# A two-layer graph attention network: layer 1's rows split among TensorE, VectorE and ScalarE by a search, its softmax moved, and the 41-row tile fetched row by row

## The chip, the cores and the metric

The kernel runs on one core of a Trainium2 chip. The metric is device time in microseconds (us) of one execution; lower is better. The engines are named as the profile names them: PE (TensorE, matmuls), DVE (VectorE), ACT (ScalarE), POOL (GpSimd, which here issues the gathers) and SP (SyncE, which issues the plain DMAs). Each engine works through its own instructions in the order in which the program lists them; semaphores order the engines against each other.

## The reference

The inputs are 10,000 nodes of 768 numbers, float32, and 170,000 edges, to which the reference adds a loop at every node. Two graph attention layers follow each other, each with a layer norm and a residual product:

```
def gat_conv(x, src, dst, W, a_src, a_dst, bias, heads, out_ch, concat):
    xl = (x @ W).reshape(n, heads, out_ch)
    alpha_src = einsum('nhc,hc->nh', xl, a_src); alpha_dst = einsum('nhc,hc->nh', xl, a_dst)
    e = leaky_relu(alpha_src[src] + alpha_dst[dst], 0.2)
    e = exp(e - segment_max(e, dst)[dst])
    alpha = e / (segment_sum(e, dst)[dst] + 1e-16)
    out = segment_sum(xl[src] * alpha[:, :, None], dst)
    ... # heads side by side (concat) or averaged
    return out + bias

h = relu(layer_norm(gat_conv(x, W1, ..., heads=4, out_ch=256, concat=True))) + x @ Wr1 + br1
h1 = h
h = layer_norm(gat_conv(h, W2, ..., heads=1, out_ch=768, concat=False)) + h1 @ Wr2 + br2
return layernorm(x + h)
```

So layer 1 has rows of 4 x 256 = 1024 numbers, layer 2 rows of 768.

## The kernel before

**Preparation and table.** The first part sorts the nodes by their number of edges and makes lists of neighbours, while PE multiplies all nodes by W1; the products, with the two logits of each head beside them, go to a table in DRAM (rows of 1033 numbers). The sorted nodes are cut into 79 tiles of 128. A tile of n rows needs n gathers: gather k fetches, for each of its 128 nodes, the table row of that node's k-th neighbour, one node on each partition. The tiles have 8 to 27 rows, and one has 41. They are worked on in the order 8, 10, 11, ... 26, 41, 27, 25, ... 9 rows; by number of tiles: one each of 8, 9, 10, 25, 26, 27 and 41 rows, three each of 11 and 12, five of 13, six of 14, eight of 15, seven of 16, eight of 17, seven each of 18 and 19, six of 20, four each of 21 and 22, two each of 23 and 24.

**Layer 1** (`ordered_layer1`) is what the change is about. Its instructions stand in the order written by hand. The gathered rows lie in a ring of 29 slots (`Ring`, `RING1`); `ring.fetch(q)` lists gathers on POOL up to row q, and a gather into a slot waits until whoever used the slot's old row is done. For each tile of up to 29 rows:

- `logits` (L477 to L489, DVE, with an exp on ACT, L485) makes the weights e of all of the tile's rows, for which all rows must have landed. `normalised` (L496 to L502, DVE) divides them by their sum. Both are called through the generator `weights_of(t + 1)` near the end of tile t: its first step, the logits, three rows before the end, its second one row later, and the rest at the start of the next tile, ahead of the table store.
- The first m rows of a tile (`on_pe`, at most `ON_PE1` = 4) are PE's: `summed` has ACT make a diagonal matrix of the weights for each row and head (L723, four a row), and PE multiplies the rows by them into `acc` in PSUM (L729; a matmul of float32 shows as two records).
- Of the other rows every fourth is DVE's alone: `weigh` multiplies and adds with four instructions (L519), onto `acc` in PSUM. The rest are shared: `multiply` has ACT multiply the row in place by its weights (L508, four instructions), running at most `LEAD` = 3 rows ahead, and DVE adds the result in one instruction (L515).
- At the start of the next tile DVE takes statistics of the finished `acc` (L572, L574), ACT makes the deviation of them (`sd`, L576 and L577), and DVE makes h in three instructions (L586, L588, L800). PE transposes x and h (L699), ACT copies the transposes out of PSUM (`xT`, `hT`, L700), and PE does the products x @ Wr1 (L171) and h @ W2 (L817). ACT copies the latter into `row` (L759), and SP stores it into layer 2's table (L761). The two halves of `row` and the transposes share two PSUM buffers (`half`).
- SP also stores h (L812) and x (L707) for layer 2; POOL gathers the next tile's x (`next_x`, `fetch_x`).

The 41-row tile doesn't fit the ring. `attend_parts` takes it in three groups of 13 or 14 rows, with a running maximum: four rows by PE into `sums`, the first third of the others by DVE alone, the rest shared; the earlier total is scaled by `fade` (L539, L542) when the maximum rises. At the end of a group DVE adds `sums` (L553), and only then the group's slots are fetched again:

```
                nc.vector.tensor_add(acc[:, :c], acc[:, :c], sums[:, :c])
                ring.fetch(hi + ring.size)
                continue
```

All work that is due in a tile (`due`: hT's copies, the product h @ W2, the next gather of x), and the product x @ Wr1, stand ahead of the first group.

**Layer 2** does the same with 768 numbers a row and a ring of 41 slots, in which every tile fits.

Of the kernel before, what the change touches and what calls it, by code (L numbers as in the profile page):

```python
# [28 lines left out]
F32 = mybir.dt.float32  # L29
# [6 lines left out]
P = 128  # L36
BANK = 512
# [10 lines left out]
RING2 = 41  # L48
LEAD = 3
DIAGONALS = 5  # L50
ON_PE2 = 512
SHARE = 4
ON_PE1 = 4
# [26 lines left out]
def gnn_kernel(ctx, tc, x, x_cols, src, dst, src_col, dst_col, W1, a_src1, a_dst1, b1, g1, be1, Wr1, br1,  # L80
# [441 lines left out]
    def attend_parts(small, ring, acc, h_, ad, bias, heads, dh, t, summed=None):  # L522
# [5 lines left out]
        top = total = None  # L528
        nc.vector.memset(acc[:, :c], 0.0)
        for lo, hi in zip(cuts, cuts[1:]):  # L530
# [5 lines left out]
            if top is not None:  # L536
                fade = small.tile([P, heads], F32, name="fade")
# [8 lines left out]
            if summed:  # L546
                sums, m = summed(lo, e)
                for q in range(lo + m, hi):
                    shared = q >= lo + m + (hi - lo - m) // 3
                    if shared:  # L550
                        multiply(ring.slot(q), e[:, q - lo], dh)
                    weigh(acc, ring.slot(q), e[:, q - lo], dh, shared=shared)
                nc.vector.tensor_add(acc[:, :c], acc[:, :c], sums[:, :c])  # L553
                ring.fetch(hi + ring.size)
                continue
            for q in range(lo, hi):
                shared = heads > 1 and (q - lo) % SHARE
                if shared:
                    multiply(ring.slot(q), e[:, q - lo], dh)
                weigh(acc, ring.slot(q), e[:, q - lo], dh, shared=shared)  # L560
                ring.fetch(q + 1 + ring.size)
        divided(small, h_, acc, total, bias, heads, dh)
# [115 lines left out]
    def ordered_layer1():  # L678
        nc.scalar.add_instruction(mybir.InstLoadActFuncSet(name=nc.get_next_instruction_name(), act_func_set_id=6, engine=nc.scalar.engine))
        with tc.tile_pool(name="b1", bufs=1) as pool, tc.tile_pool(name="small1", bufs=2) as small, \  # L680
# [5 lines left out]
            def fetch_x(t):  # L686
                xt = pool.tile([P, D0], F32, name="xt")
                gather(xt, x[:, :], nodes(t))
                return xt
# [13 lines left out]
            def from_x(t):  # L703

                xT = pool.tile([P, K0, P], F32, name="xT")
                moves = halves(xT, xt)
                nc.sync.dma_start(x_d[t], xt)  # L707
                return xT, moves
# [5 lines left out]
            def on_pe(t):  # L714


                return min(max(SLOTS[t] // 2 - 5, 1), ON_PE1, SLOTS[t])

            def summed(acc, diagonals, e, q, lo, hi, m):

                for k in range(lo, hi):
                    for i in range(H1):
                        nc.scalar.activation(diagonals[:, k * H1 + i, :], ident, AF.Copy,  # L723
                                             scale=e[:, k, i:i + 1])
                for k in range(lo, hi):
                    for i in range(H1):

                        c, d = i * DH1, (i + 1) * DH1
                        nc.tensor.matmul(acc[:, c:d], diagonals[:, k * H1 + i, :], ring.slot(q + k)[:, c:d],  # L729
                                         start=(k == 0 and c % BANK == 0),  # L730
                                         stop=(k == m - 1 and (d % BANK == 0 or d == C1)),
                                         skip_group_check=True)

            def weights_of(t):
# [6 lines left out]
                diagonals = pool.tile([P, ON_PE1 * H1, P], F32, name="diagonals")  # L741
                for lo, hi in ((0, min(m, 2)), (min(m, 2), m)):
                    summed(acc, diagonals, e, FIRST[t], lo, hi, m)
                    yield acc

            def shared(t, k):
                return (k - on_pe(t)) % SHARE > 0

# [19 lines left out]
            for t in range(NT + 1):  # L768
# [4 lines left out]
                if whole and not ready:  # L773
                    ahead = weights_of(t)
                    ready += itertools.islice(ahead, 2)
# [8 lines left out]
                if whole:  # L784
                    e, acc = ready
                if last:
                    r_before, means = last
                    stats = deviation(small, pieces(means[:, :C1], BANK))
                for _ in ahead:
                    pass  # L790
# [16 lines left out]
                if live and t:  # L807
                    r = product(xT, wr1, C1, ps_r)
# [26 lines left out]
                if live and not whole:  # L835
                    due(n)
# [4 lines left out]
                    def some(q, e):  # L841
                        m = min(ON_PE1, e.shape[1])
                        diagonals = pool.tile([P, ON_PE1 * H1, P], F32, name="diagonals")
                        summed(sums, diagonals, e, q, 0, m, m)
                        return sums, m

                    h = pool.tile([P, C1], F32, name="h")
                    attend_parts(small, ring, h, acc, ad, None, H1, DH1, t, some)
                ready = []
                ahead = iter(())  # L850
                if whole and t + 1 < NT and SLOTS[t + 1] + LEAD <= ring.size:
                    ahead = weights_of(t + 1)
                for k in range(n if whole else 0):
                    multiplied(k + 1 + LEAD)
                    if n - LEAD <= k < n - LEAD + 2:
                        ready += itertools.islice(ahead, 1)
# [5 lines left out]
                ready += itertools.islice(ahead, max(2 - len(ready), 0))  # L862
# [5 lines left out]
    def ordered_layer2():  # L868
        nonlocal ps_big
        with tc.tile_pool(name="b2", bufs=1) as pool, tc.tile_pool(name="small2", bufs=2) as small, \  # L870
# [61 lines left out]
            def residual(t):  # L932
# [4 lines left out]
                for c in range(0, C2, BANK):  # L937
# [3 lines left out]
                    for j in range(K1):  # L941
                        nc.tensor.matmul(r[:, c:d], hT[:, j, :], wr2[:, j, c:d], start=False,  # L942
                                         stop=(j == K1 - 1 and (d < C2 or not whole(t))),
# [340 lines left out]
```

## Time and profile before

| | |
|---|---|
| median of 7 runs | 5656.28 us (5637.28 to 5664.47) |
| the profiled execution | 5655.13 us, its span 5653.3 us |
| busy in the span | PE 4900.7 us (87%), DVE 4287.8 (76%), POOL 3228.4 (57%), PE's weight loads 2898.2 (51%), ACT 2810.3 (50%) |
| layer 1, by its first gather and its last tile's statistics | 892 to 3429 us from the span's start |
| moved by DMA | 1591.37 MB, mean 281 GB/s |
| DVE adds of shared rows, L515 | 801, mean 1230 ns |
| ACT multiplications, L508 | 3284, mean 508 ns (they overlap: 1338.2 us in all) |

Times are of one profiled execution, in us from the start of the span unless ns is said. In a list of groups or a timeline a line has the kernel's line, the engine, the operation, the tiles written and read, their shapes, the number of instructions, and in brackets the idle time of the engine just before, with what ended it. A stretch's line has its length, then for each engine busy us and the number of instructions, the clock that was granted to PE (1.00 is full), the mean busy share of the 16 DMA engines and GB/s. In the slices each digit is the busy share of one fortieth of the span, in tenths.

### The profile page before, as it was taken

How to read it: one execution, taken by the hardware profiler on the slowest of the kernel's cores; microseconds unless marked ns; L12 is line 12 of the kernel's file. 1: busy time of each engine (PE TensorE's matmuls, PEld its weight loads, DVE VectorE, ACT ScalarE, POOL GpSimd, SP SyncE). 2: the span in 40 equal slices, each digit the busy share in tenths (PEclk: the TensorE clock that was granted, in tenths of full speed). 3: DMA queues.
4: the chain of work that ended last, by engine and by line, in shares of the span. 5: the costliest groups of instructions: out<-in, count | busy, mean ns of one | idle time of the engine just before them, and what ended most of it. 6: DMA issues, size and time to landing. Idle time of an engine off the chain costs nothing. (4 is left out here: it accounts for less than half of the span.)

```text
span 5653.3 us, 59565 instructions
## 1 busy us (share of the span) xinstructions
PE 4900.7 (87%) x15188; PEld 2898.2 (51%) x15191; DVE 4287.8 (76%) x7729; ACT 2810.3 (50%) x8184; POOL 3228.4 (57%) x3159
## 2 busy tenths in 40 slices
PE   9999996999999865789999998998887747788898
PEld 3444443555555543455555555655555534455565
DVE  5783344999999886888899995886676656767787
ACT  3443344777787766777877762332222222222232
POOL 3447364556666655566665543666666656656663
PEclk9999997999999987899999999998888877888999
DMA  4333636999999986899999986998888878888885
GB/s 155 122 98 86 92 93 248 321 335 352 362 368 368 346 319 229 319 344 353 358 360 358 340 287 252 325 333 305 295 304 286 285 242 299 297 295 299 313 326 195
DMA packets 474306, 1591.37 MB, mean 281 GB/s; under 512 B 118327, under 2 KB 122487, under 8 KB 473958
## 3 DMA queue, kind: packets, MB, share of 16 engines
q0 software_dynamic: 322384, 1286.62, 64.3%
q1 hardware_dynamic: 149520, 297.43, 16.1%
q10 hardware_dynamic: 2054, 3.42, 0.2%
q8 instruction: 128, 2.10, 0.1%
q14 instruction: 220, 1.80, 0.1%
HBM read 1431.80 MB, written 177.29 MB: 285 GB/s over the span
## 5 line engine op out<-in xcount | busy, mean ns | idle before, releaser
L424 POOL DMA_INDIRECT ring<-table,slots x2675 | 2649.8, 991 | 1744.1 <-issue 527.6
L519 DVE SCALAR_TENSOR_TENSOR acc<-ring,e,acc 128x512 f32<-128x512 f32 (+1 forms) x2530 | 1578.0, 624 | 150.6 <-PE acc L729 48.7
L508 ACT ACTIVATE ring<-ring,e 128x256 f32<-128x256 f32 x3284 | 1338.2, 508 | 2.4 <-issue 2.2
L515 DVE TENSOR_TENSOR acc<-acc,ring 128x1024 f32<-128x1024 f32 x801 | 985.6, 1230 | 72.3 <-ACT ring L508 2.1
L942 PE MATMUL big<-wr,w 128*128 128x512 f32 (+1 forms) x2464 | 896.9, 508 | 161.1 <-issue 159.1
L928 PE MATMUL big<-ring,diagonals 128*128 128x256 f32 x2754 | 731.2, 424 | 189.9 <-issue 152.5
L171 PE MATMUL big<-w,xT 128*128 128x512 f32 x1896 | 827.4, 598 | 26.9 <-DMA w<-in_W_dram 10.0
L171 PE MATMUL big<-wr,xT 128*128 128x512 f32 x1896 | 834.8, 597 | 0.2 <-ACT xT L700 0.2
L817 PE MATMUL half<-w,hT 128*128 128x512 f32 (+1 forms) x2528 | 830.4, 486 | 0.0
L942 PEld LDWEIGHTS big<-wr,w 128*128 128x128 f32 x2464 | 487.6, 199 | 541.9 <-issue 510.0
L928 PEld LDWEIGHTS big<-ring,diagonals 128*128 128x128 f32 x2754 | 581.5, 214 | 343.1 <-issue 213.6
L927 ACT ACTIVATE diagonals<-ident,e 128x128 f32<-128x128 f32 x1377 | 423.9, 388 | 647.5 <-remote 274.4
L729 PE MATMUL acc<-ring,diagonals 128*128 128x256 f32 x1912 | 483.0, 411 | 220.6 <-ACT diagonals L723 200.5
L817 PEld LDWEIGHTS half<-w,hT 128*128 128x128 f32 x2528 | 477.8, 189 | 372.8 <-issue 327.2
L171 PEld LDWEIGHTS big<-w,xT 128*128 128x128 f32 x1896 | 362.9, 192 | 487.4 <-issue 469.6
L171 PEld LDWEIGHTS big<-wr,xT 128*128 128x128 f32 x1896 | 357.4, 192 | 421.3 <-issue 420.6
L729 PEld LDWEIGHTS acc<-ring,diagonals 128*128 128x128 f32 x1912 | 389.9, 207 | 306.1 <-ACT diagonals L723 218.5
L576 ACT ACTIVATE sd<-mv,eps 128x1 f32<-128x1 f32 x237 | 69.3, 293 | 706.4 <-DVE mv L574 450.2
L723 ACT ACTIVATE diagonals<-ident,e 128x128 f32<-128x128 f32 x956 | 292.8, 387 | 202.8 <-DVE e L499 138.6
L660 DVE TENSOR_TENSOR scr<-big,ad_b 128x1024 f32<-128x1024 f32 x79 | 96.7, 1224 | 381.5 <-ACT row L657 325.9
L665 POOL TENSOR_TENSOR row<-row,none 128x1024 f32<-128x1024 f32 x79 | 186.9, 2366 | 268.3 <-ACT row L657 264.9
L485 ACT ACTIVATE e<-e 128x68 f32<-128x68 f32 (+29 forms) x160 | 38.2, 239 | 574.3 <-DVE e L484 283.7
(172 smaller groups left out, 3629.6 us busy)
## 6 DMA issues: line engine op xcount, KB each, us to landing
ring<-table,slots POOLq DMA_INDIRECT x2675
table<-row SPq DMA_DIRECT2D x79, 516.0 KB
h_d<-hT SPq DMA_DIRECT2D x79, 512.0 KB
w<-h_d SPq DMA_DIRECT2D x77, 512.0 KB
table<-row SPq DMA_DIRECT2D x79, 385.0 KB
ring<-table SPq DMA_DIRECT2D x79, 385.0 KB
xT<-in_x_cols_dram SPq DMA_DIRECT2D x79, 384.0 KB
x_d<-xt SPq DMA_DIRECT2D x79, 384.0 KB
```

Source lines behind the costliest of these rows:

```text
L171: nc.tensor.matmul(p[:, c:e], aT[:, j, :], w[:, j, c:e], start=(j == 0), stop=(j == k - 1))
L424: nc.gpsimd.indirect_dma_start(out=to, out_offset=None, in_=table, in_offset=bass.IndirectOffsetOnAxis(ap=index, axis=0), **more)
L508: nc.scalar.activation(row[:, s], row[:, s], AF.Copy, scale=e[:, h:h + 1])
L515: nc.vector.tensor_add(acc[:, :c], acc[:, :c], row[:, :c])
L519: nc.vector.scalar_tensor_tensor(acc[:, s], row[:, s], e[:, h:h + 1], (acc if first is None else first)[:, s], op0=OP.mult, op1=OP.add)
L665: nc.gpsimd.tensor_add(row[:, :C1], row[:, :C1], b1_b)
L723: nc.scalar.activation(diagonals[:, k * H1 + i, :], ident, AF.Copy, scale=e[:, k, i:i + 1])
L729: nc.tensor.matmul(acc[:, c:d], diagonals[:, k * H1 + i, :], ring.slot(q + k)[:, c:d], start=(k == 0 and c % BANK == 0), stop=(k == m - 1 ...
L817: nc.tensor.matmul(q, hT[:, j, :], w2[:, j, c:c + q.shape[1]], start=(j == 0), stop=(j == K1 - 1))
L927: nc.scalar.activation(diagonals[:, k % G, :], ident, AF.Copy, scale=e[:, k, :])
L928: nc.tensor.matmul(to, diagonals[:, k % G, :], ring.slot(FIRST[t] + k)[:, ON_PE2:C2], start=False, stop=(k == n - 1), skip_group_check=True)
L942: nc.tensor.matmul(r[:, c:d], hT[:, j, :], wr2[:, j, c:d], start=False, stop=(j == K1 - 1 and (d < C2 or not whole(t))), skip_group_check= ...
```

## The change

In layer 1 a search replaces the fixed shares. For every number n of rows it tries all splits into rows of PE (`pe`), rows of DVE alone (`alone`) and shared rows (`both`), and takes the one with the least longest time of three linear costs:

```
+PE_FIXED, PE_ROW = 24.0, 1.86
+DVE_FIXED, DVE_ROW, DVE_SUM = 7.9, 2.15, 1.31
+ACT_FIXED, ACT_ROW, ACT_DIAGONAL = 4.0, 1.65, 1.21
...
+            def balanced(n):
+                def longest(pe, alone):
+                    both = n - pe - alone
+                    return max(PE_FIXED + PE_ROW * pe, DVE_FIXED + DVE_SUM * both + DVE_ROW * alone,
+                               ACT_FIXED + ACT_DIAGONAL * pe + ACT_ROW * both)
+                return min(((pe, alone) for pe in range(1, n) for alone in range(1, n - pe + 1)),
+                           key=lambda s: (longest(*s), s))
...
             def on_pe(t):
-                return min(max(SLOTS[t] // 2 - 5, 1), ON_PE1, SLOTS[t])
+                return split[SLOTS[t]][0]
...
             def shared(t, k):
-                return (k - on_pe(t)) % SHARE > 0
+                m, alone = split[SLOTS[t]]
+                return (k - m) * alone % (SLOTS[t] - m) >= alone
```

`summed` becomes a generator that does two rows a step, with two buffers of two rows' diagonals in place of one buffer of four rows'. The steps of `weights_of(t + 1)` are called at other rows:

```
+                begin = n
                 if whole and t + 1 < NT and SLOTS[t + 1] + LEAD <= ring.size:
+                    begin = min(max(n - EARLY, n + SLOTS[t + 1] - ring.size + EARLY), n - 2)
                     ahead = weights_of(t + 1)
                 for k in range(n if whole else 0):
                     multiplied(k + 1 + LEAD)
-                    if n - LEAD <= k < n - LEAD + 2:
-                        ready += itertools.islice(ahead, 1)
+                    if k == begin or k > begin + 1:
+                        step = list(itertools.islice(ahead, 1))
+                        ready += step[:2 - len(ready)]
```

(`EARLY` is 5.) At a tile's start, when its first sums were begun in the tile before, the rest of its diagonals and the first multiplications now stand ahead of the statistics; otherwise the normalisation and all sums stand behind them:

```
-                if whole:
+                if len(ready) == 2:
                     e, acc = ready
+                    for _ in ahead:
+                        pass
+                    multiplied(first + 2)
                 if last:
                     r_before, means = last
                     stats = deviation(small, pieces(means[:, :C1], BANK))
+                if whole and len(ready) < 2:
+                    if not ready:
+                        ahead = weights_of(t)
+                    ready += itertools.islice(ahead, 2 - len(ready))
+                    e, acc = ready
                 for _ in ahead:
                     pass
```

In the 41-row tile PE takes the last four rows of a group (the first four in the last group); `sums` is added in the next group, behind its logits; each row is fetched again as soon as it is listed as used; and the product x @ Wr1 stands behind group 1, the rest of the due work behind group 2 (`between`):

```
             if top is not None:
+                nc.vector.tensor_add(acc[:, :c], acc[:, :c], sums[:, :c])
...
+            m = min(ON_PE1, hi - lo - 1)
+            pe = lo if hi == cuts[-1] else hi - m
+            sums, steps = summed(e[:, pe - lo:], pe, m)
+            next(steps)
+            if pe == lo:
+                for _ in steps:
+                    pass
+            alone = [q for q in range(lo, hi) if not pe <= q < pe + m]
+            for k, q in enumerate(alone):
+                shared = k >= len(alone) // 3
                 if shared:
                     multiply(ring.slot(q), e[:, q - lo], dh)
+                if k == len(alone) // 3 + 1:
+                    for _ in steps:
+                        pass
                 weigh(acc, ring.slot(q), e[:, q - lo], dh, shared=shared)
                 ring.fetch(q + 1 + ring.size)
-        divided(small, h_, acc, total, bias, heads, dh)
+            ring.fetch(hi + ring.size)
+            between.pop(0)()
+        nc.vector.tensor_add(acc[:, :c], acc[:, :c], sums[:, :c])
+        divided(small, h_, acc, total, None, heads, dh)
```

SP's store of x moves from the next tile's start (`from_x`) to just behind the gather that fetches it (`fetch_x`):

```
             def fetch_x(t):
                 xt = pool.tile([P, D0], F32, name="xt")
                 gather(xt, x[:, :], nodes(t))
+                nc.sync.dma_start(x_d[t], xt)
                 return xt
...
-                moves = halves(xT, xt)
-                nc.sync.dma_start(x_d[t], xt)
-                return xT, moves
+                return xT, halves(xT, xt)
```

In layer 2 the branches for tiles that don't fit its ring go, which no tile took.

## The prediction

> **What bounds the kernel now.** I read the page's forty slices first, to find layer 1; then the busy times by stretches, cut where a tile's first statistics (L572) start, so that each stretch holds whole tiles; then DVE's idle time inside a tile; then ACT, PE and POOL in order of time.
>
> ```profile
> span 5653.3 us, 59565 instructions
> ...
> DVE  5783344999999886888899995886676656767787
> ...
> DMA  4333636999999986899999986998888878888885
> ```
> Layer 1 is about slices 6 to 24 (141 us each): DVE and DMA both show 8 or 9, with a dip in slice 15, where the 41-row tile stands.
>
> ```profile
> core 0: us, PE busy (x) PEld busy (x) DVE busy (x) ACT busy (x) POOL busy (x), PEclk, DMA share, GB/s
> 1096.80:1174.90 78.10, 76.73 (x256) 44.55 (x255) 72.52 (x118) 60.47 (x160) 45.99 (x46) 1.00 0.94 339
> 1174.90:1287.90 113.00, 106.40 (x351) 62.10 (x350) 104.66 (x174) 80.19 (x213) 65.30 (x65) 0.98 0.94 335
> 1402.10:1520.30 118.20, 112.53 (x385) 67.39 (x384) 109.76 (x179) 91.13 (x244) 74.65 (x72) 1.00 0.98 360
> 1520.30:1610.90 90.60, 88.15 (x305) 53.69 (x304) 82.56 (x135) 71.89 (x195) 58.97 (x57) 1.00 1.00 365
> 1910.60:2079.70 169.10, 125.55 (x408) 77.14 (x407) 137.47 (x213) 120.02 (x320) 94.91 (x95) 0.86 0.88 321
> 2121.50:2269.10 147.60, 83.10 (x273) 54.65 (x274) 101.87 (x193) 88.30 (x243) 74.34 (x70) 0.77 0.62 222
> ```
> These are three tiles of 14 rows (26.0 us each), four of 15 (28.2), four of 17 (29.6), three of 18 (30.2), four of 22 to 24 (42.3), and the tiles of 41 and 27 rows together. Up to 17 rows DVE is 92 to 93% busy, and the rest is steps under 0.15 us between its instructions: DVE alone sets the period. At 18 to 20 rows DMA is at 0.99 to 1.00 as well. From 22 on DVE waits, and in the last stretch 45.7 of 147.6 us are idle on DVE.
>
> ```profile
> 1403.67 0.29 ACT L576 ACTIVATE sd<-mv,eps 128x1 f32<-128x1 f32 x1 [2.31 <-DVE mv L574]
> ...
> 1412.49 11.29 ACT L508 ACTIVATE ring<-ring,e 128x256 f32<-128x256 f32 x28
> ...
> 1428.33 2.44 ACT L723 ACTIVATE diagonals<-ident,e 128x128 f32<-128x128 f32 x8 [2.38 <-DVE total L498]
> ```
> ACT in one 17-row tile: a row's four multiplications cost 1.61 us (11.29 / 7), a row's four diagonals 1.22, and ACT idles some 7 us in a tile of 29.6, 2.31 and 2.38 of it here. That slack is what the change spends.
>
> ```profile
> 1989.24 9.19 PE L729 MATMUL acc<-ring,diagonals 128*128 128x256 f32 x32 [8.83 <-ACT diagonals L723]
> ...
> 1998.47 2.06 DVE L519 SCALAR_TENSOR_TENSOR acc<-ring,e,acc 128x256 f32<-128x256 f32 x4 [1.13 <-PE acc L729]
> ...
> 2162.50 7.19 PE L729 MATMUL acc<-ring,diagonals 128*128 128x256 f32 x32 [3.63 <-ACT fade L539]
> ```
> Four rows' sums take PE 7.19 us, 1.8 a row, and 9.19 after a long idle time, when the granted clock is 0.5 for a while. DVE adds its rows onto PE's sums in PSUM, so its first row waits for all of them.
>
> ```profile
> 2153.95 0.99 POOL L424 DMA_INDIRECT ring<-table,slots  x1 [22.58 <-PE acc L729]
> ...
> 2158.91 1.22 DVE L553 TENSOR_TENSOR h<-h,acc 128x1024 f32<-128x1024 f32 x1 [11.39 <-PE acc L729]
> ...
> 2210.37 0.25 DVE L477 TENSOR_TENSOR e<-ring 128x88 f32<-128x88 f32 x1 [6.90 <-DMA ring<-table,slots]
> 2215.17 0.18 DVE L477 TENSOR_TENSOR e<-ring 128x20 f32<-128x20 f32 x1 [4.56 <-DMA ring<-table,slots]
> ```
> In the 41-row tile DVE waits 11.39 us for the sums of its first group (PE does two products ahead of them), POOL holds back all fetches for 22.58, and so the next tile's rows come 11.5 late.
>
> **Rows shared out by a search (tiles of 8 to 27 rows).** A row is PE's (four diagonals, four matmuls), DVE's alone (L519: 2.06 us and a step, 2.16), or shared (ACT multiplies, 1.61; DVE adds, 1.30: three in 3.91). The formula in the diff gives, as PE/alone/shared, old to new: 13 rows 1/3/9 to 1/1/11; 14: 2/3/9 to 1/1/12; 15: 2/4/9 to 1/1/13; 16: 3/4/9 to 2/1/13; 17: 3/4/10 to 2/2/13; 18: 4/4/10 to 3/2/13; 19: 4/4/11 to 3/2/14; 22: 4/5/13 to 5/3/14; 24: 4/5/15 to 6/4/14; 26: 4/6/16 to 7/5/14. On DVE this saves, in us a tile, 1.7 (13), 0.4 (14), 1.3 (15 and 16), 0.4 (17 to 19), 3.0 to 4.8 (22 to 27). If all of it came off the end, tiles of 12 to 17 rows would give 39 us.
>
> It does not, since ACT and DVE then form a ring. The chain of a tile: DVE's mean and variance; ACT's sd 0.44, row copies 0.73, xT copies 0.75 and some 0.5 for PE's transposes (they need the PSUM halves that the row copies free, and the multiplication that stood between is moved ahead of sd), hT copies 0.94, the multiplications of all shared rows but two, exp 0.36; then DVE's normalisation 1.12, three rows 3.91, statistics 1.64. That is 10.4 + 1.61 x (shared - 2): 28.1 at 13 shared, 26.5 at 12, 24.9 at 11. So 13 rows go from 26.0 to 24.9, 14 from 26.0 to 26.5, 15 from 28.2 to 28.1, 16 from 28.3 to 28.1, 17 to 29.15 (DVE's), 12 by -0.6 (PE's products bound it). At 18 to 21 I take -0.2 at 19 and nothing else: DMA is full there, and at 20 and 21 the diagonals (up to 4.9) and a multiplication now stand ahead of sd on ACT, so DVE waits 2 to 3 us for sd where it saves 0.9 to 1.7 and a PE wait of about 1. With 3, 5, 6, 8, 7, 8 and 7 tiles (12 to 17, and 19): -1.8 - 5.5 + 3.0 - 0.8 - 1.4 - 3.2 - 1.4 = **-11**; ends -39 (all of DVE's saving) and +33 (rival below).
>
> One rule bears on the tiles at 0.99 to 1.00. The Trainium skill, DMA: Bandwidth & Descriptors, Specifications, sets about 358 GB/s of HBM for a core; Perfetto Trace Analysis, Roofline, lets a lone core go to about 435. The 18-row tile moves some 11 MB (365 GB/s x 30.2 us), so an estimate from these pages is 31 us by the first and 25 by the second; the second would give the tiles of 18 to 20 rows DVE's 0.4 us each. The rows here, 365 to 367 at a full share, lie just over the first, and I keep them full.
>
> **Softmax moved.** Logits start five rows before a tile's end instead of three where the next tile has up to 19 rows, four before at 20, three at 21, two from 22 on. The same instructions are issued; what moves is which wait stands where. From 22 rows on only the logits are early: normalisation, all diagonals and all of PE's sums now come after the tile's statistics. DVE's first row can start at 1.6 (statistics) + 1.25 (normalise) + 0.6 (first diagonals) + 1.8 x PE rows + 2.0 (PE cold, 9.19 - 7.19) + 0.2: 14.65 us at 5 PE rows, 16.45 at 6, 18.25 at 7, where it is 6.8 now. Behind that wait stand all of DVE's rows, and POOL's fetches into their slots. Adding the rows and 1.4 of logits: 22 rows 40.7 (now 39.7 on average, from one tile's statistics to the next), 23: 42.0 (41.9), 24: 44.7 (42.9), 25: 46.0 (45.0), 26: 47.2 (41.8, no logits). The row waits on DMA there now (up to 4.8 before L477) I take as gone. With 4, 2, 2, 1, 1 tiles: **+14**; ends 0 (PE warm, sums under the h steps) and +25 (the row waits stay).
>
> **The 41-row tile and the 27-row one after it.** Sums are added a group later, with PE's two products set between groups: -11.4. Fetching row by row, the 27 rows are issued while groups 2 and 3 run: of 11.5 I take -9, since group 3's PE rows are freed only behind the second product (10.5). The 27-row tile has seven PE rows for four: +5.4; DVE's own rows -4.8; its wait of 3.05 for the next rows goes. Sum some **-22**; ends -10 and -30.
>
> **Store of x moved** from the next tile's start to just behind the gather. SP now waits there for the gather; queued behind it is only the next table store, due most of a tile later. POOL's waits of some 2.1 us a tile for that store go at 17 to 20 rows, where queued rows hide them: **0**, down to -10. In layer 2 only unused branches go: 0.
>
> **Sum.** -11 + 14 - 22 = -19 on the profiled execution's 5655.1 (span 5653.3 and 1.8 around it): 5636; the median of the runs is 1.2 above the profiled one, so 5637.
>
> **Rivals.** (1) *ACT's ring has more slack than I give it*, since ACT can run ahead: tiles of 12 to 17 rows give 39, not 11: 5609. For it: ACT's 7 us of idle time; against: ACT at 1.61 a row cannot catch up with DVE at 1.30 in a run of 13. (2) *Slower: xT's copies wait for PE.* One row shows ACT waiting 1.76 us for the transposes in a 15-row tile, with a multiplication ahead to hide part of it; if the 0.5 in my chain is 1.76, the 26 tiles of 13 to 16 rows lose 33: 5670. It decides from about 1.2 us of wait on. (3) *The 41-row tile's fetches are held by PE's rows*: PE's sums of group 3 stand behind the second product and the next tile's logits still wait; the pair gives 10: 5649. (4) *The big tiles lose nothing*: 5623.
>
> **How the numbers follow.** A measurement of this kernel can tell about 0.2%, 11 us, from no change. Chances: forecast 0.40, (1) 0.17, (2) 0.20, (3) 0.13, (4) 0.10. Faster by over 11 us: (1), (4) and three quarters of the forecast, 0.57; slower by over 11: most of (2) and a little more, 0.21; within: 0.22. The range goes from 5604, a little under (1), to 5672, a little over (2).
>
> **What would show it.** Right: tiles of 13 rows near 24.9 us, of 15 and 16 still near 28 with ACT's idle time down to 2 or 3 us; before DVE's first row of a 22- to 26-row tile a wait of 7 to 11 us for PE's acc; no wait at the group add in the 41-row tile, and the pair at 147.6 less about 22. Wrong: 15-row tiles at 27 (ring slack) or 29 and more (transposes); no PE wait in the big tiles; a row wait of over 5 us after the 41-row tile; any change of layer 2's length.

## The result, and the profile after

The changed kernel takes 5696.44 us (median; 5686.95 to 5720.22), the kernel before 5656.75 on the same chip: a ratio of 1.0072, interval 1.0062 to 1.0082. It is slower, by 40 us, where 19 faster was forecast, and it lies outside the range of 5604 to 5672.

The profiled execution has a span of 5695.2 us, 41.9 more than before. Layer 1 (from its first gather to its last tile's statistics) takes 2586.4 us for 2537.3, so it grows by 49.1; the part ahead is 1.1 shorter, layer 2 6.1 shorter. The forecast's terms and the trace go by a tile's number of rows. The table has the sums, each tile counted from the statistics that open it to the next ones, and the first tile from the first gather:

| rows (tiles) | before | after | difference | forecast |
|---|---|---|---|---|
| 8 to 19 (57) | 1626.3 | 1635.1 | +8.8 | -11 |
| 20 and 21 (10) | 348.2 | 362.4 | +14.2 | 0 |
| 22 to 26 (10) | 415.2 | 457.8 | +42.6 | +14 |
| 41 and 27 (2) | 147.6 | 131.1 | -16.5 | -22 |

The slices of the page, in the order span, DVE, DMA, answer to the first fence of the prediction:

```profile
span 5695.2 us, 59340 instructions
...
DVE  5883344888988767678999885887766757767787
...
DMA  4333637899999887889999995998888878888885
```

Counting slices from 0, DVE shows 7, 6, 6 and 7 in slices 13, 14, 16 and 17, where it showed 8: these are the big tiles on both sides of the dip. The dip itself, slice 15, is shallower (DVE and DMA 7 for 6). And in slices 7 to 12, all but slice 10, DVE shows 8 where it showed 9. The stretches of the prediction's second fence, cut at the new times, with four tiles of 16 rows besides (so: three tiles of 14 rows, four of 15, four of 16, four of 17, three of 18, four of 22 to 24, the tiles of 41 and 27):

```profile
core 0: us, PE busy (x) PEld busy (x) DVE busy (x) ACT busy (x) POOL busy (x), PEclk, DMA share, GB/s
1094.50:1178.50 84.00, 79.35 (x257) 45.62 (x256) 71.99 (x102) 70.77 (x183) 44.53 (x46) 0.98 0.91 326
1178.50:1290.40 111.90, 100.27 (x301) 55.15 (x300) 101.15 (x142) 101.17 (x264) 64.21 (x65) 0.94 0.92 334
1290.40:1406.80 116.40, 108.25 (x347) 62.41 (x346) 101.46 (x146) 105.26 (x278) 69.98 (x69) 0.96 0.96 346
1406.80:1525.20 118.40, 109.37 (x356) 63.48 (x355) 108.65 (x159) 105.80 (x279) 72.46 (x73) 0.97 0.98 361
1525.20:1615.00 89.80, 84.63 (x292) 51.20 (x291) 81.89 (x121) 82.79 (x220) 58.74 (x58) 1.00 0.99 369
...
1925.40:2110.50 185.10, 137.14 (x448) 86.97 (x448) 125.97 (x186) 129.75 (x348) 93.98 (x95) 0.87 0.82 294
2156.90:2288.00 131.10, 85.13 (x292) 56.98 (x292) 96.01 (x182) 86.58 (x239) 77.04 (x70) 0.81 0.70 248
```

In the 14-row tiles DVE is busy 72.0 us for 72.5, in the 15-row ones 101.2 for 104.7, and ACT 70.8 for 60.5 and 101.2 for 80.2. The share moved as planned, but the 14-row tiles take 84.0 for 78.1, and the four tiles of 22 to 24 rows 185.1 for 169.1 with 11.5 us less work on DVE. What became longer is waits, so I counted DVE's idle times above 0.15 us over all tiles of a size, by the line that waited and what it waits for:

| DVE, us | busy | PE's acc (L519, L523) | rows by DMA (L477, L481) | sd (L588, L597) | ACT's multiplication (L515, L519) | ACT's exp (L506) |
|---|---|---|---|---|---|---|
| 13 to 19, before | 1270.8 | 9.0 | 3.3 | 0.5 | 2.3 | 0 |
| after | 1244.4 | 0.7 | 8.8 | 0 | 22.5 | 28.1 |
| 20 and 21, before | 309.3 | 11.2 | 3.6 | 0 | 0.3 | 0 |
| after | 297.5 | 4.9 | 6.7 | 20.1 | 14.0 | 0 |
| 22 to 26, before | 349.1 | 16.0 | 21.4 | 0 | 2.1 | 0 |
| after | 319.8 | 87.4 | 17.4 | 0 | 9.9 | 0 |

(Where two lines stand, the first is the kernel before's. The steps between instructions, under 0.15 us each, are 3 to 10 us less after, since there are fewer instructions. The profile puts some of the waits in the last two columns down to DVE's own row before, or to nothing it shows.)

**A 24-row tile.** DVE's timeline, with idle time and what ended it in brackets:

```profile
2059.63 1.29 DVE L581 BATCH_NORM_STATS2 st<-acc 128x6 f32<-128x512 f32 x2
...
2065.03 1.22 DVE L827 SCALAR_TENSOR_TENSOR h<-h,big 128x1024 f32<-128x1024 f32 x1
2076.55 2.06 DVE L523 SCALAR_TENSOR_TENSOR acc<-ring,e,acc 128x256 f32<-128x256 f32 x4 [10.31 <-PE acc L751]
...
2106.26 0.26 DVE L481 TENSOR_TENSOR e<-ring 128x96 f32<-128x96 f32 x1 [4.81 <-DMA ring<-table,slots]
```

The first row starts 16.9 us after the statistics; 16.45 was forecast. But the wait for the next rows, which the forecast let go, is there all the same, 4.81. POOL's gathers in the same tile, and two stretches of it (the wait for PE, and a stretch after it), show what that wait does to the transfers:

```profile
2066.87 0.99 POOL L428 DMA_INDIRECT ring<-table,slots  x1 [6.01 <-PE acc L751]
2069.86 0.99 POOL L428 DMA_INDIRECT ring<-table,slots  x1 [2.00 <-PE acc L751]
```
```profile
2064.60:2076.00 11.40, 11.40 (x44) 9.50 (x43) 1.53 (x2) 7.34 (x23) 4.90 (x5) 0.81 0.50 131
2090.00:2100.00 10.00, 9.37 (x30) 5.29 (x28) 9.30 (x13) 9.56 (x24) 6.36 (x7) 1.00 1.02 415
```

While DVE waits for PE, the slots of PE's rows come free one per PE row, so POOL issues five gathers in 11.4 us and DMA moves 131 GB/s, a third of the 415 that it moves once the rows are let go. So the wait for PE holds transfers back. It would be natural to put the 4.81 us at the tile's other end down to that, too; the runs below speak against it (see "The row waits over all runs").

**A 16-row tile.** ACT, then PE:

```profile
1291.99 0.29 ACT L585 ACTIVATE sd<-mv,eps 128x1 f32<-128x1 f32 x1 [1.07 <-DVE st L581]
...
1296.63 0.86 ACT L710 COPY xT<-half 128x512 f32<-128x512 f32 x2 [3.37 <-PE half L709]
...
1303.12 12.88 ACT L512 ACTIVATE ring<-ring,e 128x256 f32<-128x256 f32 x32
```
```profile
1288.63 4.07 PE L849 MATMUL half<-w,hT 128*128 128x512 f32 x17
1292.54 3.62 PE L751 MATMUL acc<-ring,diagonals 128*128 128x256 f32 x16
1295.99 0.82 PE L709 MATMUL half<-ident,xt 128*128 128x128 f32 x6
```

ACT waits 3.37 us for PE's transposes of x, which stand on PE behind the product h @ W2 and the sums. This tile takes 30.8 us; the next one of 16 rows takes 27.9, with a wait of 0.47 there. So it goes on: tiles of 14 rows come at 26.2 to 26.7 or at 27.5 to 29.7, of 13 at 24.6 to 24.8 or 26.2 to 26.4. Why it is about every second tile no run here shows.

**A 21-row tile and the 27-row tile.** DVE in both:

```profile
2515.90 1.28 DVE L595 SCALAR_TENSOR_TENSOR h<-acc,mv,g 128x1024 f32<-128x1024 f32 x1
2520.00 1.28 DVE L597 SCALAR_TENSOR_TENSOR h<-h,sd,be 128x1024 f32<-128x1024 f32 x1 [2.82 <-ACT sd L586]
```
```profile
2184.23 1.21 DVE L541 TENSOR_TENSOR h<-h,acc 128x1024 f32<-128x1024 f32 x1
...
2229.40 0.25 DVE L481 TENSOR_TENSOR e<-ring 128x88 f32<-128x88 f32 x1 [0.96 <-DMA ring<-table,slots]
2234.42 0.18 DVE L481 TENSOR_TENSOR e<-ring 128x20 f32<-128x20 f32 x1 [4.76 <-DMA ring<-table,slots]
```

In the 21-row tile the step that uses sd waits 2.82 us, since the rest of the diagonals and a multiplication now stand ahead of sd on ACT; over the ten tiles of 20 and 21 rows these waits are the 20.1 of the table, and before there were none. The group add of the 41-row tile (L541, L553 before) waits for nothing now, where it waited 11.39. The 27 rows behind it are late by 0.96 + 4.76 = 5.7 us, where it was 6.90 + 4.56 = 11.5.

### The profile page after: what moved, and what is told of

It reads as the page before. It is cut to its first block, busy times and chain, and to the rows that moved or that the text cites. A ratio compares the mean times of both kernels' runs of the same rounds, so it can differ in the third digit from the quotient of the medians.

```text
span 5695.2 us, 59340 instructions
## 1 busy us (share of the span) xinstructions
PE 4892.9 (86%) x14988; PEld 2881.2 (51%) x14991; DVE 4203.7 (74%) x7277; ACT 3072.3 (54%) x8820; POOL 3226.9 (57%) x3159
## 5 line engine op out<-in xcount | busy, mean ns | idle before, releaser
L512 ACT ACTIVATE ring<-ring,e 128x256 f32<-128x256 f32 x4020 | 1644.8, 505 | 2.3 <-issue 2.3
L523 DVE SCALAR_TENSOR_TENSOR acc<-ring,e,acc 128x512 f32<-128x512 f32 (+1 forms) x1894 | 1267.4, 669 | 194.8 <-PE acc L751 111.8
L519 DVE TENSOR_TENSOR acc<-acc,ring 128x1024 f32<-128x1024 f32 x985 | 1211.9, 1230 | 122.1 <-ACT ring L512 26.7
L175 PE MATMUL big<-wr,xT 128*128 128x512 f32 x1896 | 860.6, 612 | 0.2 <-issue 0.2
L959 ACT ACTIVATE diagonals<-ident,e 128x128 f32<-128x128 f32 x1377 | 425.2, 388 | 629.0 <-remote 308.1
L751 PE MATMUL acc<-ring,diagonals 128*128 128x256 f32 x1712 | 438.8, 417 | 215.9 <-ACT diagonals L745 208.3
L175 PEld LDWEIGHTS big<-w,xT 128*128 128x128 f32 x1896 | 362.4, 192 | 487.1 <-issue 468.1
L175 PEld LDWEIGHTS big<-wr,xT 128*128 128x128 f32 x1896 | 368.9, 198 | 437.4 <-issue 437.3
L751 PEld LDWEIGHTS acc<-ring,diagonals 128*128 128x128 f32 x1712 | 358.3, 211 | 289.2 <-ACT diagonals L745 219.8
L672 ACT ACTIVATE scr<-scr 128x256 f32<-128x256 f32 x632 | 253.6, 403 | 120.3 <-DVE scr L669 120.3
L745 ACT ACTIVATE diagonals<-ident,e 128x128 f32<-128x128 f32 x856 | 260.4, 390 | 90.1 <-DVE e L503 55.1
```

The lines of the kernel that those rows point to most:

```text
L175: nc.tensor.matmul(p[:, c:e], aT[:, j, :], w[:, j, c:e], start=(j == 0), stop=(j == k - 1))
L512: nc.scalar.activation(row[:, s], row[:, s], AF.Copy, scale=e[:, h:h + 1])
L519: nc.vector.tensor_add(acc[:, :c], acc[:, :c], row[:, :c])
L523: nc.vector.scalar_tensor_tensor(acc[:, s], row[:, s], e[:, h:h + 1], (acc if first is None else first)[:, s], op0=OP.mult, op1=OP.add)
L672: nc.scalar.activation(m[:, s], m[:, s], AF.Copy, accum_out=row[:, C1 + i * H1 + h:C1 + i * H1 + h + 1])
L745: nc.scalar.activation(diagonals[:, (k - lo) * H1 + i, :], ident, AF.Copy, scale=e[:, k, i:i + 1])
```

## The experiments

They ran on other chips, on which layer 2 is some 300 us shorter (the kernel before takes 5341 to 5352 us there) and layer 1 about as long (e3, close to the changed kernel, 2578.8 for 2586.4); so ratios to the kernel before on the same chip, and lengths of layer 1's tiles, are compared. Each kernel has one trace. In the column of 8 to 19 rows two things limit that: on the other chips the first two tiles take some 69 us, for 74.7 before and 72.3 changed in the table's first two rows; and e6, e9 and e10, which do in these tiles what the changed kernel does, come out 8 to 15 us under it (5 to 11 without the first two tiles). The sums by tile size of all of them, as above:

| kernel | ratio (interval) | 8 to 19 | 20, 21 | 22 to 26 | 41 and 27 |
|---|---|---|---|---|---|
| before | 1 | 1626.3 | 348.2 | 415.2 | 147.6 |
| changed | 1.0072 (1.0062 to 1.0082) | 1635.1 | 362.4 | 457.8 | 131.1 |
| e1 softmax put back | 1.0027 (1.0016 to 1.0037) | 1645.5 | 351.0 | 422.7 | 134.6 |
| e2 shares put back | 1.0052 (1.0038 to 1.0065) | 1612.4 | 364.5 | 450.8 | 128.9 |
| e3 store of x put back | 1.0074 (1.0060 to 1.0087) | 1638.1 | 362.2 | 447.0 | 131.5 |
| e4 the 41-row part alone | 0.9968 (0.9958 to 0.9979) | 1618.2 | 352.8 | 417.6 | 132.2 |
| e5 order at a tile's start put back | 1.0087 (1.0073 to 1.0101) | 1634.4 | 360.1 | 453.9 | 132.2 |
| e6 sums early | 1.0086 (1.0071 to 1.0100) | 1626.8 | 373.6 | 448.4 | 132.9 |
| e7 parts by size | 0.9955 (0.9941 to 0.9968) | 1612.6 | 347.0 | 418.0 | 131.7 |
| e8 and ACT's cost as measured | 0.9915 (0.9902 to 0.9929) | 1592.1 | 347.5 | 416.4 | 132.6 |
| e9 first half of the sums early | 1.0009 (1.0000 to 1.0018) | 1622.8 | 354.0 | 430.4 | 133.4 |
| e10 logits alone early | 1.0154 (1.0141 to 1.0167) | 1620.3 | 397.1 | 463.5 | 132.9 |

**e1: softmax put back.** The changed kernel with the places and the order at a tile's start of before:

```
-                if len(ready) == 2:
+                if whole and not ready:
+                    ahead = weights_of(t)
+                    ready += itertools.islice(ahead, 2)
+                if whole:
                     e, acc = ready
-                    for _ in ahead:
-                        pass
-                    multiplied(first + 2)
...
-                    if k == begin or k > begin + 1:
-                        step = list(itertools.islice(ahead, 1))
-                        ready += step[:2 - len(ready)]
+                    if n - LEAD <= k < n - LEAD + 2:
+                        ready += itertools.islice(ahead, 1)
```

> The changed kernel (5696.4 us) with the softmax and the order at a tile's start put back as they were before; the new shares, the 41-row tile's new handling and the moved store of x stay. Theory A (the place: from 20 rows on PE's sums, or the deviation, now stand where DVE must wait for them): sums start two rows ahead of a tile's end again, DVE's wait before its first row falls from 8 to 10 us to about 4 in the tiles of 22 to 26 rows and its wait for sd at 20 and 21 rows goes; some 45 us come back, 5650. Theory B (the shares: too many rows on PE and ACT): the waits only move, within 10 us of the changed kernel, 5690 to 5700.

From 20 rows on most of the loss goes: 422.7 for 457.8 and 351.0 for 362.4. The tiles up to 19 rows get worse by 10: 14 rows 27.5 to 27.8 each, 15 and 16 rows 29.1 to 29.3, with no alternation. So the ratio shows some 25 us back and not the 45 of the first theory. So the place of softmax, with the order at a tile's start, is what hurts the big tiles and what helps the small ones.

**e2: shares put back.**

```
-                return split[SLOTS[t]][0]
+                return min(max(SLOTS[t] // 2 - 5, 1), ON_PE1, SLOTS[t])
...
-                m, alone = split[SLOTS[t]]
-                return (k - m) * alone % (SLOTS[t] - m) >= alone
+                return (k - on_pe(t)) % SHARE > 0
```

> The changed kernel with the old shares (PE at most 4 rows, every fourth other row DVE's alone); softmax, 41-row tile and store of x stay as changed. Theory A: PE's four sums still stand behind the statistics in the tiles of 22 rows and more, DVE's first row starts at 12.9 us in place of 14.7 to 18.3 but DVE has 3 to 5 us more of rows, so these tiles stay where they are; only the small tiles give back 5 to 15 us: 5680 to 5692. Theory B: the tiles return to their old periods and the 41-row tile's gain is left: 5635.

The reverse, as the first theory has it: the tiles up to 19 rows fall to 1612.4 (1618.2 with old shares and old places, e4), by more than the 5 to 15 it named, and the big ones keep their loss (450.8). The searched shares cost the small tiles 23 us against the old ones in the same places (26 against e3 on the same chip, 8 to 14 against e6, e9 and e10), and the big ones nothing that can be told: 457.8 changed and 447.0 in e3, on both sides of 450.8.

**e3: store of x put back** to the next tile's start:

```
                 gather(xt, x[:, :], nodes(t))
-                nc.sync.dma_start(x_d[t], xt)
                 return xt
...
+                nc.sync.dma_start(x_d[t], xt)
```

> The changed kernel with the store of x put back to the next tile's start. Theories A and B: within 6 us of the changed kernel (5690 to 5702), since the queued rows hide the wait on POOL. If the store in its new place is what delays transposes or gathers (theory C): 10 us or more faster, below 5686.

The ratio is 1.0074: the store's place is worth nothing that can be told. In this one trace the tiles of 22 to 26 rows wait 7.5 us for rows, for 17.4, and take 10.8 less; whether that is the store's doing is not shown.

**e4: the 41-row part alone**, that is e1, e2 and e3 together.

> The kernel before with only the new handling of the 41-row tile (sums added a group later, row-by-row fetch, products between groups); shares, softmax and store of x as before. All theories: the 41-row tile's period falls by about 26 us as in the changed kernel, and the 27-row tile, with four PE rows, stays near 51 or loses up to 5 to a row wait: 5630 to 5636, against 5656.8. If the gain is lost later to the tiles behind it: 5645 or more.

0.9968, and layer 1 2520.9 us: this part gains 15.4 on its pair of tiles, nearly as in the full change (the 41-row tile itself falls by 15.6 and not by the 26 expected; in the full change it falls by 26.5, and the 27-row tile takes 61.1 for 51.1), and at 20 to 26 rows there are 7 us over the row of before, 8 under it below (6.4 of the 8 in the first two tiles).

**e5: the order at a tile's start put back.** Only the remaining diagonals and the first two multiplications go behind sd again:

```
                 if len(ready) == 2:
                     e, acc = ready
-                    for _ in ahead:
-                        pass
-                    multiplied(first + 2)
```

> The changed kernel, but at a tile's start the rest of the diagonals and the first two multiplications of shared rows stand behind the statistics, sd and the row copies again; when logits, exp, normalisation and the first sums start (five rows before the end) stays as changed, and so do the shares. Theory A (the order on ACT at a tile's start makes the losses below 22 rows: diagonals and multiplications ahead of sd make DVE wait at 20 and 21 rows, and the multiplication that is gone from between the row copies and xT's copies no longer covers PE's transposes at 14 to 16): the ten tiles of 20 and 21 rows come to about 351 us from 362, the alternation of 14- and 16-row tiles goes, and the tiles up to 19 rows come to about 1625 from 1635; tiles of 22 to 26 rows stay at 450 to 458; layer 1 falls by some 20 us and the ratio is about 1.003. Theory B (the ring of ACT and DVE sets the small tiles in any order, and a multiplication put back into it lengthens it): tiles of 15 and 16 rows go from 28.5 to about 29.1, the small tiles to about 1645, and the ratio stays at 1.006 or more.

Neither theory holds alone. The alternation goes as the first says; ACT no longer waits for the transposes:

```profile
1285.38 0.29 ACT L585 ACTIVATE sd<-mv,eps 128x1 f32<-128x1 f32 x1 [2.66 <-DVE mv L583]
...
1286.54 1.71 ACT L512 ACTIVATE ring<-ring,e 128x256 f32<-128x256 f32 x4
1288.15 0.85 ACT L710 COPY xT<-half 128x512 f32<-128x512 f32 x2
```

A multiplication covers them, but it now stands in the ring, and every tile of 15 and 16 rows takes 28.8 to 29.1, as the second says. The two cancel: 1634.4. At 20 and 21 rows the wait for sd goes (20.1 to 0) and DVE waits for PE's sums in its place (4.9 to 23.3): 360.1, where 351 was expected.

**e6: sums early.** Logits one to three rows earlier than changed where the next tile has 20 to 25 rows:

```
-                    begin = min(max(n - EARLY, n + SLOTS[t + 1] - ring.size + EARLY), n - 2)
+                    begin = min(max(n - EARLY, n + SLOTS[t + 1] - ring.size + 1), n - 2)
```

> The changed kernel with one number altered: the next tile's logits start no later than before in the ring's terms but up to four rows earlier at 20 to 25 rows (n + next - 28 in place of n + next - 24, at least five from the end), so that normalisation, diagonals and PE's sums of the next tile start ahead of its statistics in tiles of 20 to 25 rows; shares as changed. The rows whose logits are read then have less time to land. Theory A (in the big tiles the place of the sums is the cause, and the waits on DMA come only from POOL's fetches being held while DVE waits for the sums): the tiles of 22 to 26 rows fall from 458 us to about 430, and those of 20 and 21 from 362 to 350 to 358; ratio about 1.002. Theory B (the rows of the next tile cannot be there earlier, so the wait on DMA ahead of the logits grows by what the wait for PE's sums loses): the tiles of 22 to 26 rows stay at 450 or more; ratio 1.006 or more.

The second theory holds, within 2 us. The wait for PE's sums falls from 87.4 to 11.5 in the tiles of 22 to 26 rows, but the wait for rows rises from 17.4 to 54.0 and the wait for sd from 0 to 38.0. Logits four or five rows before the end ask for rows that have not landed.

**e7: parts put together by tile size.** Old shares; new places under 20 rows, old ones from there on:

```
+                early = whole and SLOTS[t] < 20
+                if early and len(ready) == 2:
...
+                    begin = n - EARLY if SLOTS[t + 1] < 20 else n - LEAD
```

> Parts put together by tile size: the 41-row part and the store of x as changed; the shares of before; the changed place of softmax only for tiles under 20 rows, and the place of before from 20 rows on. If the parts add by size, layer 1 is 1612 (up to 19 rows, as with the shares put back) + 353 (20 and 21) + 418 (22 to 26) + 131 (27 and 41, both as with the 41-row part alone) + 7 = about 2521 less the six of the small tiles, 2515, against 2537 before: ratio 0.994 to 0.997. If the stages borrow from one another (queued rows), it is no better than the 41-row part alone: 0.997 or more.

0.9955, with layer 1 at 2509.3: the parts add by size.

**e8: the same with the search under 20 rows, on measured costs** (ACT's diagonals are counted at nothing, and PE's costs are lower, too):

```
-PE_FIXED, PE_ROW = 24.0, 1.86
+PE_FIXED, PE_ROW = 22.6, 1.85
-ACT_FIXED, ACT_ROW, ACT_DIAGONAL = 4.0, 1.65, 1.21
+ACT_FIXED, ACT_ROW, ACT_DIAGONAL = 8.0, 1.61, 0.0
```

> As the kernel put together by size, but the tiles under 20 rows take their shares from the search with ACT's fixed cost as the ring of ACT and DVE shows it (8.0 and 1.61 a shared row, no diagonals; PE 22.6 and 1.85 a row): PE/alone/shared 1/2/10 at 13 rows, 2/1/11 at 14, 2/2/11 at 15, 2/2/12 at 16, 3/2/12 at 17, 3/2/13 at 18, 4/2/13 at 19. Theory A (the loss of the searched shares was only that ACT's fixed cost, 4.0, left out the wait of ACT for DVE and of DVE for ACT): tiles of 15 rows come to 26.6 to 27.2 from 28.0, of 14 to about 25.9, of 16 and 17 to 28 and 29; the small tiles to about 1597, and the ratio to about 0.992. Theory B (at 15 to 19 rows DMA at 0.98 to 1.00 holds the period whatever DVE saves): small tiles at 1612 or more, as in the kernel put together by size.

0.9915, the fastest kernel here: 1592.1 up to 19 rows. 15 rows take 26.7 (28.3 before), 16 rows 28.0, 17 rows 28.3 (29.5). Only 14 rows miss, at 26.6 for 25.9, which they take with the old shares. DMA did not hold the tiles of 15 to 17 rows. Four 17-row tiles in e7, on the same chip with the old shares, and then in e8 four of 17 rows and three of 18:

```profile
1387.60:1506.10 118.50, 113.01 (x390) 68.82 (x390) 109.82 (x178) 91.65 (x246) 71.56 (x72) 1.00 0.98 361
```
```profile
1383.60:1497.30 113.70, 110.97 (x381) 67.05 (x380) 103.73 (x154) 103.64 (x277) 73.17 (x73) 1.00 0.99 376
1497.30:1587.30 90.00, 86.37 (x293) 52.15 (x292) 81.75 (x120) 83.08 (x221) 58.86 (x58) 0.98 1.00 371
```

**e9: first half of the sums early.** Where the next tile has 20 to 26 rows, logits three rows before the end, normalisation and two rows' sums one row later, as before the change; the order at the start as changed:

```
+                    if SLOTS[t + 1] >= 20:
+                        begin = n - LEAD
...
-                    if k == begin or k > begin + 1:
+                    late = whole and t + 1 < NT and SLOTS[t + 1] >= 20
+                    if k == begin or (k == begin + 1 if late else k > begin + 1):
```

> The changed kernel, but where the next tile has 20 to 26 rows its logits start three rows before the end, as before the change, and normalisation with the diagonals and PE's sums of the first two rows follows one row later; the order at a tile's start, the shares and all other places stay as changed. Putting back place and order at the start together gave 423 us for the tiles of 22 to 26 rows and 351 for those of 20 and 21, putting back the order alone 454 and 360. Theory A (the loss of the big tiles is that none of PE's sums, or the first ones too late, lie ahead of the statistics): about 425 to 432, and 350 to 358 at 20 and 21 rows, where some wait for sd stays since the other diagonals stand ahead of it; ratio about 1.002. Theory B (place and order at the start act only together: with the sums ahead of it, DVE's sd waits behind the diagonals of the later PE rows and the gain is given back): 440 or more, with a wait of some 5 us at the first step that uses sd; ratio 1.004 or more.

The first theory holds in its times: 430.4 and 354.0, ratio 1.0009. The wait that the second foretold comes as well: in a 24-row tile DVE waits for sd, which stands on ACT behind the later rows' diagonals, and not for PE. At the end of the tile it waits for the next rows, 6.67 us for 4.81 in the changed kernel:

```profile
2042.47 1.28 DVE L597 SCALAR_TENSOR_TENSOR h<-h,sd,be 128x1024 f32<-128x1024 f32 x1 [5.94 <-ACT sd L586]
...
2045.01 2.06 DVE L523 SCALAR_TENSOR_TENSOR acc<-ring,e,acc 128x256 f32<-128x256 f32 x4
...
2075.48 0.26 DVE L481 TENSOR_TENSOR e<-ring 128x96 f32<-128x96 f32 x1 [6.67 <-DMA ring<-table,slots]
```

The first row starts 11.4 us after the statistics (at 2033.61) for 16.9. Over the tiles of 22 to 26 rows the wait for PE's sums goes from 87.4 to 0, the wait for sd comes to 52.0, and the row waits rise from 17.4 to 33.3.

**e10: logits alone early.** As e9, but only the logits and exp stand ahead of the statistics:

```
-                    if k == begin or k > begin + 1:
+                    if k == begin or (False if late else k > begin + 1):
```

> As the run before, but where the next tile has 20 to 26 rows only the logits and exp are put back to three rows before the end (one row earlier than changed at 22 rows and more); normalisation and all of PE's sums come after the tile's statistics. Theory A (the sums' place is the cause, not the logits'): tiles of 22 to 26 rows stay at 445 to 460, and those of 20 and 21 rows, whose sums now come later too, rise from 362 to 375 or more; ratio 1.007 to 1.012. Theory B (the logits' one row is the cause: they stand in the way of the last rows' additions, and exp comes later): 22 to 26 rows fall to 430 or less and the ratio to about 1.003.

The first theory again, and further than expected: 463.5, and the tiles of 20 and 21 rows, whose sums now come late too, take 397.1 for 362.4; their waits for PE's sums rise from 4.9 to 59.3. Logits one row earlier give nothing back (row waits at 22 to 26 rows are 25.7 for 17.4); the sums' place does.

**The row waits over all runs.** At 22 to 26 rows they go by the place of the logits. Where these stand two rows before the end, as changed (in one tile of nine three rows), the row waits come to 17.4, and in e2, e3 and e5 to 13.2, 7.5 and 15.0; where they stand three rows before it, to 21.4 in the kernel before and 24.7 to 33.3 in e1, e4, e7, e8, e9 and e10; in e6, mostly four or five rows before it, to 54.0. They do not go by the wait for PE: e9 and e10 differ only in where normalisation and the sums stand, and the wait for PE's sums is 0 in e9 and 85.4 in e10, the row waits 33.3 and 25.7. A likely reason is the ring: the last rows of the next tile are fetched into slots that come free in the last rows of this one, and in e9 a gather takes 6.9 us from issue to landing (median), some five of DVE's shared rows at 1.30.

## Why the prediction was wrong, point by point

Several of the signs that the prediction named for being right did come: a wait for PE of 7.5 to 10.5 us before the first row of every tile of 22 to 26 rows, no wait at the group add, tiles of 15 rows near 28. They stood for terms that the sum had priced; it was wrong by waits that it had left out.

**22 to 26 rows (+14 forecast, +42.6 measured): the mechanism was right, two terms of the sum were left out.** The wait for PE's sums, 14.65 to 18.25 us to the first row, came as worked out (16.9 for 16.45). The step that failed is "The row waits on DMA there now (up to 4.8 before L477) I take as gone": they are 17.4 us of 21.4 still. The other is that a row that ACT multiplies is ready when DVE comes to it: 9.9 us of waits for ACT, 7.8 more than before, had no term. 17.4 + 9.9 are 27.3 of the 28.6 missed. The upper end given for this term, +25 "the row waits stay", was the better value and still too low: all 21.4 on top of +14 would have been +35. e1, e9 and e10 show the place of the first sums as the cause of the wait for PE. The row waits have another: they go by the logits, which the change moves by only one row there, and not by the gathers that are held during the wait for PE (e9 against e10).

**20 and 21 rows (0 forecast, +14.2 measured).** The wait for sd was forecast at 2 to 3 us a tile and came to 20.1 for ten; DVE's work fell by 11.8 and the PE wait by 6.3, both about as counted. What was left out is again the wait for ACT's multiplications, 0.3 before and 14.0 after: a 21-row tile has 14 shared rows for 12 and three of DVE's own between them for five, and DVE at 1.30 us a shared row catches up with ACT at 1.61.

**Up to 19 rows (-11 forecast, +8.8 measured).** ACT's ring was right in its undisturbed tiles: 27.9 at 13 shared rows (28.1 forecast), 26.2 to 26.7 at 12 (26.5), 24.6 to 24.8 at 11 (24.9). The term that failed is "some 0.5 for PE's transposes": it is 0.5 to 0.9 in some tiles of 13, 14 and 16 rows and 1.7 to 3.4 in the others, and 13 and 16 rows come out 0.7 above the forecast on average, 14 rows 0.9. That is rival (2), with its mechanism and above its 1.2, but only in about every second tile and hardly in the 15-row ones (0.47 to 0.70 in seven of eight), so it cost some 14 (5 x 0.7 + 6 x 0.9 + 7 x 0.7) and not 33. The rest of the miss is spread: 12, 17 and 19 rows gained 2.2 and not 6.4, and the tiles of 8 to 11 lost 1.8. What DVE saves in the tiles of 13 to 19 rows (26.4 of work, some 10 of steps) is paid for by waits for ACT (28.1 on exp, 20.2 more on multiplications). e5 shows that the cover cannot be had for nothing: the multiplication that hides the transposes lengthens the ring by 1.0. All this is one trace: without the first two tiles the changed code takes 1562.8 here and 1551.5 to 1558.0 in e6, e9 and e10, the code of before 1551.6, and 1549.9 in e4. So the loss at these sizes is 0 to 13 us, and the gain of 11 came in none of them.

What the forecast did not see is that the new place alone, with the old shares, is worth 5.8 us there (e2 against e4, and e7, with the same code at these sizes, repeats it); DVE's waits for PE's acc are 2.2 in e2 at 13 to 19 rows, where they were 9.0.

**The 41- and 27-row tiles (-22 forecast, -16.5 measured).** The group add's wait went (11.4) as forecast. The 27 rows come 5.7 late and not 2.5, and the 27-row tile's wait for the rows after it, forecast to go, is still 3.01 (3.05 before). These two make 6.2, for 5.5 missed. The part gains in e4 without the rest.

**The store of x (0) and layer 2 (0)** were right, by e3 and by layer 2's 6 us (0.3% of it).

**The full DMA share as a limit** is not what a share of 0.99 to 1.00 shows. The forecast kept the rows at 365 to 367 GB/s; e8 moves 371 in the 18-row tiles and 376 in the 17-row ones at a share of 0.99 to 1.00, where e7 on the same chip moves 361 at 0.98 in 17-row tiles, and the 10 us above reach 415. For the 18-row tiles themselves the forecast of no change held (30.4 us before, 30.3 after), and whether DMA would hold them is open: e8 saves them only 0.4 us of DVE's work against e7, and both take 29.8. The Trainium skill, DMA: Bandwidth & Descriptors, Specifications, gives two figures, some 358 for a core's part of HBM and 435 for the fabric; the runs lie over the first and under the second.

Why was the sign wrong? The three losses have one form. The sum took work off DVE and priced only the one wait that the change plainly adds; each tile size had a second one: below 22 rows the waits for ACT, whose work grew, and from 22 rows on the row waits, which were there before and stayed.

## What to carry to other kernels

A search over shares is as good as its costs: with ACT's fixed cost at 4.0 it made the tiles up to 19 rows slower than the old shares did in the same places, and with 8.0, the chain as one engine waits for the other, it made them 1.3% faster (e8 against e7). e8 alters PE's costs and the diagonals' as well, so the fixed cost by itself is not shown. Softmax early pays while the ring has free rows, and costs as soon as the first part of the sums falls behind the statistics; so choose the place by tile size. A wait that stands in the profile now is only gone after a change if what makes it is gone: here the row waits hung on where the logits stand, the change moved those by one row, and the forecast struck the waits out.

## What was not expected of the hardware

A mean DMA share of 0.99 to 1.00 is no ceiling: at 0.98 to 1.00 the stretches of layer 1 moved 361, 365, 371 and 376 GB/s with the same kind of gathers, the last two on another chip, and 415 at 1.02 for 10 us. PE's sums of six rows in the 24-row tile took 13.70 us after 12.55 us of idle time on PE (from 2062.82 on, a granted clock of 0.81 over most of it; 2.3 a row), where four rows took 7.19 in the prediction's fence (1.8 a row).
